# Self-attention's instructions kept in the order of the program, with the first scores ahead of the first values and the comparisons spread over its tiles

## The chip, the core and the metric

The kernel runs on one core of a Trainium2 chip: TensorE (PE, with its weight loads shown apart as PEld), VectorE (DVE), ScalarE (ACT), GpSimd (POOL) and the DMA queues, each with its own list of instructions, tied together by semaphores. The metric is the device time of one execution in microseconds (us), as the median of several runs. A profile comes from one further execution; its span is the time from the first to the last instruction.

## The reference

One layer of a Perceiver: cross-attention, causal self-attention and a feed-forward network whose weights are reduced to -1, 0 and 1, each added to `x` (32 sequences of 64 rows of 512 numbers, all float32). The change lies in the second part and in what prepares the third:

```python
def _L0_attn_ref(x, WQ, WK, WV, WO):
    NUM_HEADS = 16
    D_K = D_MODEL // NUM_HEADS
    ...
    Q, K, V = (heads(WQ), heads(WK), heads(WV))
    score = jnp.einsum('bhqd,bhkd->bhqk', Q, K) / jnp.sqrt(jnp.asarray(D_K, x.dtype))
    score = score + mask
    score = score - jnp.max(score, axis=-1, keepdims=True)
    score = jnp.exp(score)
    score = score / jnp.sum(score, axis=-1, keepdims=True)
    out = jnp.einsum('bhqk,bhkd->bhqd', score, V)
    return out.transpose(0, 2, 1, 3).reshape(B, S, E) @ WO
...
h = jnp.einsum('btd,hd->bth', x, absmean(W_fc))
h = layernorm(jax.nn.gelu(h, approximate=False), ln_w, ln_b)
return jnp.einsum('bth,dh->btd', h, absmean(W_proj))
...
x = x + _L0_attn_ref(_layernorm(x, axis=-1), L0_attn_WQ, L0_attn_WK, L0_attn_WV, L0_attn_WO)
x = x + _L0_ffn_ref(_layernorm(x, axis=-1), L0_ffn_W_fc, L0_ffn_ln_w, L0_ffn_ln_b, L0_ffn_W_proj)
```

`absmean` divides a weight matrix by its mean magnitude and rounds to -1, 0 or 1. In the kernel this is two comparisons of each weight with a threshold.

## The kernel before

`x` stays in SBUF as 16 tiles of 128 rows (two sequences each, `xs[0]` to `xs[15]`). The stages follow each other: queries of the cross-attention, cross-attention (`cross_last`), then `rest`, which holds `self_attention` and `feed_forward`.

Self-attention takes two tiles as a group (GA = 2, eight groups). For a group, `centred_group` normalises the rows of both tiles (`centred`, L107: statistics, mean and variance, scale on DVE, the inverse root on POOL, then `xn` on DVE); `turned_group` transposes them on PE (`atp`) and ACT copies them to SBUF (`axT`). `heads` makes queries, keys and values of a group in six steps: `turned` for half of WQ (`aWQ`, copied by ACT to `QT`), half of WK (`aWK`, copied by DVE to `KT`), and the values of one tile (`aV`, copied by ACT to `V`), and the same once more. It is a generator, and the loop over the tiles takes one of its steps at a time, for the group after the one that is being attended to.

A tile passes through `exponentials` (PE: 16 small products for the scores `sc`; DVE: two operations that scale and mask them into `s`, and the row maximum `amx`; POOL: subtract it; ACT: the exponential), `normalise` (DVE: row sum `atot`, reciprocal, multiply), `turn` (PE: transposes `aptp`; ACT and DVE copy them out to `wo`, whose storage holds the turned probabilities), `mix` (PE: `po`; ACT: `aoT`) and `self_out` (PE: `aout`; DVE adds it to `xs`). The scores of tile i + 1 are made inside tile i, between `mix` and `self_out`.

Two other kinds of work are laid between the tiles. `compare` makes the ternary weights: a DMA on SP's queue fetches one of 32 pieces (`raw_q`, 128x512, in a pool `raw` of two buffers), and two DVE instructions compare it (L869 and L870) into `wf` (first 16 pieces) or `wp`. Three pieces stand in each of the tiles 0 to 10. `ffn_input` (L898) normalises a tile for the feed-forward network (`xn_f`), transposes it on PE (`ftp`) and splits it on DVE into a high and a low part (`fxh`, `fxl`); the first four stand at the end of tiles 5, 7, 9 and 11. In tiles 14 and 15, which have no further group, the steps are the first twelve products of the feed-forward network (`first_hidden`, `fh`; ACT: GELU and square; POOL: sums).

Buffers that matter: `norm` (L90) has two for `xn`, shared by the normalised rows of every stage; `s`, `xT` and `aoT` have one each; the PSUM pool `as_m` has three for all of `aWQ`, `aWK`, `aV`, `atp`, `aptp`, `aout`, `ftp` and `fh`; the scores' PSUM has one [...].

What sets the order: the program is written tile by tile, but the framework's scheduler, when it builds the program, puts each engine's instructions in an order of its own that keeps all dependencies. [...] In the program before, the scheduler moves work forward where it expects an engine to be free: the list of DVE has all 32 pieces compared by the middle of tile 5, row statistics of later groups stand in the cross-attention, and the scores of a tile are often issued in two parts.

Of the kernel before, what the change touches and what calls it, by code (L numbers as in the profile page):

```python
# [18 lines left out]
F32 = mybir.dt.float32  # L19
# [5 lines left out]
ALU = mybir.AluOpType  # L25
# [3 lines left out]
P = 128  # L29
B, T, D = 32, 64, 512  # L30
S = 1601
NT = B * T // P
# [6 lines left out]
GA = 2  # L39
GT = 4  # L40
FC = FF // P
# [39 lines left out]
def perceiver_kernel(ctx: ExitStack, tc: tile.TileContext, a: dict, out: bass.AP):  # L81
    nc = tc.nc
# [6 lines left out]
    small = ctx.enter_context(tc.tile_pool(name="small", bufs=4))  # L89
    norm = ctx.enter_context(tc.tile_pool(name="norm", bufs=2))  # L90
# [16 lines left out]
    def centred(src, gain, eps, name):  # L107

        stats = small.tile([P, 6], F32, tag="stats", name=f"stats_{name}")
        nc.vector.bn_stats(stats, src)  # L110
        mv = small.tile([P, 2], F32, tag="mv", name=f"mv_{name}")
        nc.vector.bn_aggr(mv, stats)
        rs = small.tile([P, 1], F32, tag="rs", name=f"rs_{name}")
        nc.vector.tensor_scalar(rs, mv[:, 1:2], gain, eps, ALU.mult, ALU.add)
        nc.gpsimd.tensor_tensor(rs, rs, neghalf[:, 0:1], ALU.pow)
        xn = norm.tile([P, D], F32, tag="xn", name=f"xn_{name}")
        nc.vector.tensor_scalar(xn, src, mv[:, 0:1], rs, ALU.subtract, ALU.mult)
        return xn

    H = HD // 2  # L120
    wkv = const.tile([P, DC, 2, HD], F32, name="wkv")
# [7 lines left out]
    with ExitStack() as st:  # L129
# [126 lines left out]
        xT = query_input(0)  # L256
# [4 lines left out]
        for g in range(B // 4):  # L261
# [8 lines left out]
            xT = after  # L270
# [612 lines left out]
    def rest(store, measured):  # L883
        st = ExitStack()
        fw = st.enter_context(tc.tile_pool(name="fw", bufs=1))
        wf = fw.tile([P, DC, FF], F32R, name="wf")
        wp = fw.tile([P, FC, D], F32R, name="wp")
        lnw = fw.tile([P, FC], F32, name="lnw")
        lnb = fw.tile([P, FC], F32, name="lnb")
        sums = fw.tile([P, 2, D], F32, name="sums")  # L890
        first = [fw.tile([P, DC, GT * P], F32R, name=f"fx{k}_0") for k in ("h", "l")]

        so_far = [None, None]

        def slot(n):
            return bank[:, n % FC // 4, n % 4 * D : (n % 4 + 1) * D]

        def ffn_input(t, to, ps_t, t_tag):  # L898
            xn = centred(xs[t], 1.0, 1e-5, f"f{t}")
            tp = ps_t.tile([P, DC, P], F32, tag=t_tag, name=f"ftp_{t}")  # L900
            for c in range(DC):
                nc.tensor.transpose(tp[:, c, :], xn[:, c * P : (c + 1) * P], ident)
            at = slice(t % GT * P, (t % GT + 1) * P)
            halves(to[0][:, :, at], to[1][:, :, at], tp)

        def hidden(n, fx, ps_m, m_tag, squares, sq_tag, adder):

            cols = slice(n % FC * P, (n % FC + 1) * P)
            ps = ps_m.tile([P, GT * P], F32, tag=m_tag, name=f"fh_{n}")
            for i, part in enumerate(fx):  # L910
                for c in range(DC):
                    nc.tensor.matmul(  # L912
                        ps,
                        wf[:, c, cols],
                        part[:, c, :],
                        start=(i == 0 and c == 0),
                        stop=(i == 1 and c == DC - 1),
                    )
            g = slot(n)
            nc.scalar.activation(g, ps, AF.Gelu)  # L920
            sq = squares.tile([P, D], F32, tag=sq_tag, name=f"fsq_{n}")
            nc.scalar.activation(sq, g, AF.Square)  # L922
            if n % FC == 0:
                so_far[:] = g, sq
            else:
                nc.gpsimd.tensor_tensor(sums[:, 0], so_far[0], g, ALU.add)  # L926
                adder.tensor_tensor(sums[:, 1], so_far[1], sq, ALU.add)  # L927
                so_far[:] = sums[:, 0], sums[:, 1]

        with ExitStack() as sa:  # L930
            done = self_attention(sa, wf, wp, first, ffn_input, hidden, measured)
        feed_forward(st, wp, lnw, lnb, sums, first, slot, ffn_input, hidden, done, store)
        st.close()

    def self_attention(st, wf, wp, first, ffn_input, hidden, measured):

        raw = st.enter_context(tc.tile_pool(name="raw", bufs=2))
        p1 = st.enter_context(tc.tile_pool(name="a1", bufs=1))
# [1 line left out]
        ps_m = st.enter_context(tc.tile_pool(name="as_m", bufs=3, space=PSUM))  # L940
# [15 lines left out]
            return wf[:, j // 4, j % 4 * D : (j % 4 + 1) * D] if j < FC else wp[:, j - FC, :]  # L956

        def centred_group(g):
            return [centred(xs[g * GA + t], 1.0, 1e-5, f"a{g}_{t}") for t in range(GA)]

        def turned_group(g, xns):
            xT = p1.tile([P, DC, GA * P], F32, tag="xT", name=f"axT_{g}")
            for t, xn in enumerate(xns):
                tp = ps_m.tile([P, DC, P], F32, tag="mm", name=f"atp_{g}_{t}")
                for c in range(DC):
                    nc.tensor.transpose(tp[:, c, :], xn[:, c * P : (c + 1) * P], ident)
                nc.scalar.copy(xT[:, :, t * P : (t + 1) * P], tp)  # L967
            return xT

        made = {}  # L970

        def heads(g, xT):


            QT = p2.tile([P, DC, GA * P], F32, tag="QT", name=f"QT_{g}")
            KT = p2.tile([P, DC, GA * P], F32, tag="KT", name=f"KT_{g}")
            V = p2.tile([P, GA, D], F32, tag="V", name=f"V_{g}")
            made[g] = QT, KT, V

            def turned(w, dst, m0, copy):  # L980
                ps = ps_m.tile([P, 2, GA * P], F32, tag="mm", name=f"a{w}_{g}_{m0}")
                for m in range(2):
                    for c in range(DC):
                        nc.tensor.matmul(  # L984
                            ps[:, m, :],
                            ws[w][:, c, (m0 + m) * P : (m0 + m + 1) * P],
                            xT[:, c, :],
                            start=(c == 0),
                            stop=(c == DC - 1),
                        )  # L990
                copy(dst[:, m0 : m0 + 2, :], ps)  # L991

            for i in range(GA):
                turned("WQ", QT, 2 * i, nc.scalar.copy)
                yield
                turned("WK", KT, 2 * i, nc.vector.tensor_copy)
                yield
                ps = ps_m.tile([P, D], F32, tag="mm", name=f"aV_{g}_{i}")
                for c in range(DC):
                    nc.tensor.matmul(  # L1000
                        ps,
                        xT[:, c, i * P : (i + 1) * P],
                        ws["WV"][:, c, :],
                        start=(c == 0),
                        stop=(c == DC - 1),
                    )
                nc.scalar.copy(V[:, i, :], ps)
                yield

        def first_hidden():  # L1010
# [82 lines left out]
            nc.vector.tensor_tensor(xs[i], ps, xs[i], ALU.add)  # L1093


        chores = {i: range(3 * i, min(3 * i + 3, 2 * FC)) for i in range(11)}
        groups = NT // GA
        xT = turned_group(0, centred_group(0))
        for _ in heads(0, xT):
            pass  # L1100
        thresholds(ps_m)
        s = exponentials(0)
        xT = turned_group(1, centred_group(1))
        xns = None
        for i in range(NT):
            g, t = divmod(i, GA)
            if t == 0:
                steps = heads(g + 1, xT) if g + 1 < groups else first_hidden()
            next(steps)
            normalise(i, s)  # L1110
            next(steps)
            if t == 0 and g + 2 < groups:
                xns = centred_group(g + 2)
            turn(i, s)
            next(steps)
            oT = mix(i)
            if i + 1 < NT:
                s = exponentials(i + 1)
            self_out(i, oT)
            for j in chores.get(i, ()):  # L1120
                compare(raw, j, piece_of(j))
            if t == GA - 1 and g + 2 < groups:
                xT = turned_group(g + 2, xns)
            if i in (5, 7, 9, 11):
                ffn_input((i - 5) // 2, first, ps_m, "mm")
        return 12

    def feed_forward(st, wp, lnw, lnb, sums, first, slot, ffn_input, hidden, done, store):
        fx = st.enter_context(tc.tile_pool(name="fx", bufs=1))
        ft = st.enter_context(tc.tile_pool(name="ft", bufs=3))  # L1130
        fq = st.enter_context(tc.tile_pool(name="fq", bufs=2))
# [1 line left out]
        ps_m = st.enter_context(tc.tile_pool(name="fs_m", bufs=2, space=PSUM))  # L1133
# [79 lines left out]
        for n in range(last):  # L1213
# [21 lines left out]
                others(g, c - 10)  # L1235
            if n in inputs_at:
                t = inputs_at[n]
                ffn_input(t, inputs[t // GT % 2], ps_t, "tp")
            if c == FC - 1:
                for t in range(GT):  # L1240
                    i = g * GT + t
# [112 lines left out]
```

## Time and profile before

| what | us |
|---|---|
| median of 3 runs | 984.78 (983.76 to 987.26) |
| the profiled execution | 985.89 |
| its span | 984.1 |
| PE busy | 906.7 (92%) |
| DVE busy | 651.9 (66%) |
| ACT busy | 306.8 (31%) |
| POOL busy | 293.1 (30%) |
| first `aWQ` of self-attention | 387.3 |
| first `fh` | 685.1 |
| last `aout` starts | 724.2 |

"Busy" is the share of the span in which an engine had an instruction running. In the rows below, a group of instructions is named by its line, engine and operation, with output <- inputs by the program's names, and the number of instructions after an x; a pair of brackets holds the time that the engine sat idle before it and what ended that. In a row of the waits, the numbers are the total in us, how often, and the longest. The costs of the instructions at hand, by their usual duration in the trace:

| instruction | engine | us each |
|---|---|---|
| `s`, one half of the rows (L1033) | DVE | 1.22 |
| `amx`, `atot` (L1042, L1051) | DVE | 1.22, 1.21 |
| normalising product (L1053) | DVE | 1.22 |
| first and second comparison (L869, L870) | DVE | 0.48, 0.75 |
| row statistics (L110) | DVE | 0.68 |
| `xn` (L117) | DVE | 0.54 |
| `fxh`, `fxl` (L876, L877) | DVE | 0.68, 0.68 |
| copy of keys (L991) | DVE | 0.69 |
| subtract of the maximum (L1043) | POOL | 1.90 |
| exponential (L1046) | ACT | 1.06 |

### The profile page before, as it was taken

To read this page: it belongs to the slowest core of one execution; us is meant where nothing else is said; L and a number is where in the kernel's file an instruction comes from. 1 tells how busy PE (TensorE), PEld (TensorE's weight loads), DVE (VectorE), ACT (ScalarE), POOL (GpSimd) and SP (SyncE) were. 2 spreads that over 40 slices of the span, in tenths; PEclk is the share of its full clock that TensorE was granted. 3 is DMA by queue.
4 is the path that set the end of the run, shared out by engine and by line. 5 is a ranking of instruction groups with operands and counts; after the bars stand their busy time and mean duration, and the time that the engine had idled before them with its cause. 6 is when DMAs were issued, how large, how long until landed. Compare 5 with 4: busy or idle time off the path is not lost.

```text
span 984.1 us, 13369 instructions
## 1 busy us (share of the span) xinstructions
PE 906.7 (92%) x4694; PEld 672.1 (68%) x4694; DVE 651.9 (66%) x1209; ACT 306.8 (31%) x694; POOL 293.1 (30%) x264
## 2 busy tenths in 40 slices
PE   4997889999999999988989999999979899999995
PEld 2786667777677766755566766766647688888884
DVE  4994456656565443499976666666439798886864
ACT  1112345455454532122222222222622233333330
POOL 3554222323222221011011111111757454443330
PEclk9999899999999999999999999999999999999998
DMA  6266664876776550023310000000000010010101
GB/s 198 65 206 168 196 190 136 278 235 206 235 208 213 149 182 24 21 86 87 87 43 1 1 1 1 1 2 1 1 1 1 1 43 1 1 44 1 43 1 46
DMA packets 60964, 83.74 MB, mean 85 GB/s; under 512 B 11060, under 2 KB 34136, under 8 KB 60888
## 3 DMA queue, kind: packets, MB, share of 16 engines
q1 hardware_dynamic: 57568, 80.60, 27.3%
q10 hardware_dynamic: 3320, 2.20, 0.7%
q8 instruction: 39, 0.64, 0.3%
q14 instruction: 37, 0.30, 0.1%
HBM read 74.38 MB, written 4.19 MB: 80 GB/s over the span
## 4 chain that ended last, share of the span: by engine, by line
PE 62%; DVE 14%; POOL 4%; issue 3%; DMA 3%; ACT 3%; SPq 1%; POOLq 0%; DVEq 0%; ACTq 0%
PE y L1225 10%; PE fh L912 10%; PE kvp L382 9%; PE aV L1000 5%; PE xo L504 5%; PE aWQ L984 4%; PE aWK L984 4%; PE lgp L424 3%; PE enc L488 3%; DVE s L1033 3%; DMA nat<-in_ctx_dram 2%; PE aout L1090 2%; PE po L1076 1%; DVE amx L1042 1%; PE sc L1028 1%
## 5 line engine op out<-in xcount | busy, mean ns | idle before, releaser
L382 PE MATMUL kvp<-wkv,ct 128*128 128x256 f32 x576 | 140.8, 391 | 4.4 <-ACT kv L389 4.4
L382 PEld LDWEIGHTS kvp<-wkv,ct 128*128 128x128 f32 x576 | 111.5, 197 | 27.9 <-issue 7.3
L926 POOL TENSOR_TENSOR sums<-sums,bank 128x512 f32<-128x512 f32 x56 | 77.2, 1378 | 90.9 <-ACT bank L920 90.7
L1225 PE MATMUL y<-wp,hTh 128*128 128x512 f32 x256 | 102.7, 401 | 0.6 <-DVE hTh L1204 0.6
L1225 PE MATMUL y<-wp,hTl 128*128 128x512 f32 x256 | 100.7, 393 | 0.7 <-DVE hTl L1205 0.7
L1043 POOL TENSOR_TENSOR s<-s,amx 128x1024 f32<-128x1024 f32 x16 | 30.6, 1913 | 226.0 <-DVE amx L1042 226.0
L920 ACT ACTIVATE bank<-fh 128x512 f32<-128x512 f32 x64 | 38.1, 599 | 154.0 <-PE fh L912 154.0
L912 PE MATMUL fh<-fxh,wf 128*128 128x512 f32 x256 | 73.1, 407 | 6.3 <-issue 4.8
L912 PE MATMUL fh<-fxl,wf 128*128 128x512 f32 x256 | 71.4, 401 | 0.0
L1033 DVE SCALAR_TENSOR_TENSOR s<-sc,cmask 64x1024 f32<-64x1024 f32 x32 | 39.1, 1222 | 44.5 <-PE sc L1028 44.1
L927 DVE TENSOR_TENSOR sums<-sums,fsq 128x512 f32<-128x512 f32 x46 | 54.6, 1186 | 19.5 <-ACT fsq L922 19.4
L1000 PE MATMUL aV<-bank,axT 128*128 128x512 f32 x128 | 62.2, 631 | 4.4 <-DVE KT L991 4.4
L389 ACT ACTIVATE kv<-kvp,rstd 128x256 f32<-128x256 f32 x72 | 33.2, 469 | 92.8 <-PE kvp L382 54.6
L504 PE MATMUL xo<-wo,encT 128*128 128x512 f32 x128 | 59.7, 609 | 2.1 <-ACT encT L497 2.0
L1090 PE MATMUL aout<-bank,aoT 128*128 128x512 f32 x128 | 59.2, 605 | 0.7 <-ACT aoT L1084 0.7
L984 PE MATMUL aWQ<-axT,bank 128*128 128x256 f32 x256 | 58.3, 381 | 1.5 <-ACT axT L967 1.5
L912 PEld LDWEIGHTS fh<-fxh,wf 128*128 128x128 f32 x256 | 47.1, 190 | 18.3 <-issue 6.8
L1205 DVE SCALAR_TENSOR_TENSOR hTl<-bank,lnw,hTh 128x512 fp32r<-128x512 f32 x64 | 55.9, 874 | 5.3 <-PE y L1225 1.1
L191 PE MATMUL q<-xT,wq 128*128 128x256 f32 x256 | 58.2, 386 | 0.0
L984 PE MATMUL aWK<-axT,bank 128*128 128x256 f32 x256 | 57.9, 379 | 0.0
L1225 PEld LDWEIGHTS y<-wp,hTh 128*128 128x128 f32 x256 | 48.2, 188 | 13.8 <-DVE hTh L1204 1.4
L912 PEld LDWEIGHTS fh<-fxl,wf 128*128 128x128 f32 x256 | 48.9, 191 | 12.5 <-issue 0.8
(156 smaller groups left out, 1625.9 us busy)
## 6 DMA issues: line engine op xcount, KB each, us to landing
nat<-in_ctx_dram SPq DMA_DIRECT2D x64, 256.0 KB, 5.1
ct<-in_ctxT_dram SPq DMA_DIRECT2D x7, 768.0 KB, 4.8
xraw<-in_x_dram SPq DMA_DIRECT2D x16, 256.0 KB, 2.7
x<-in_x_dram SPq DMA_DIRECT2D x32, 128.0 KB, 4.9
qs<-bank SPq DMA_DIRECT2D x32, 128.0 KB, 3.1
raw_g<-in_W_fcT_dram SPq DMA_DIRECT2D x16, 256.0 KB, 3.7
raw_g<-in_W_projT_dram SPq DMA_DIRECT2D x16, 256.0 KB, 4.4
raw_q<-in_W_fcT_dram SPq DMA_DIRECT2D x16, 256.0 KB, 3.0
```

What stands on the lines that cost most here:

```text
L191: nc.tensor.matmul(ps.rearrange("p b t -> p (b t)"), wq[:, c, h, :], xT[:, c, :], start=(c == 0), stop=(c == DC - 1),)
L382: nc.tensor.matmul(ps.rearrange("p k h -> p (k h)"), cts[p][:, c, j * P : (j + 1) * P], wkv[:, c].rearrange("p k h -> p (k h)"), start=(c ...
L504: nc.tensor.matmul(o, encT[:, h].rearrange("p s t -> p (s t)"), wo[:, h, :], start=(h == 0), stop=(h == NH - 1),)
L912: nc.tensor.matmul(ps, wf[:, c, cols], part[:, c, :], start=(i == 0 and c == 0), stop=(i == 1 and c == DC - 1),)
L926: nc.gpsimd.tensor_tensor(sums[:, 0], so_far[0], g, ALU.add)
L927: adder.tensor_tensor(sums[:, 1], so_far[1], sq, ALU.add)
L984: nc.tensor.matmul(ps[:, m, :], ws[w][:, c, (m0 + m) * P : (m0 + m + 1) * P], xT[:, c, :], start=(c == 0), stop=(c == DC - 1),)
L1000: nc.tensor.matmul(ps, xT[:, c, i * P : (i + 1) * P], ws["WV"][:, c, :], start=(c == 0), stop=(c == DC - 1),)
L1033: nc.vector.scalar_tensor_tensor(s[half], sc[half, :, :, half].rearrange("p r m k -> p (r m) k"), DK**-0.5, cmask[half].unsqueeze(1).to_br ...
L1090: nc.tensor.matmul(ps, oT[:, c, :], ws["WO"][:, c, :], start=(c == 0), stop=(c == DC - 1))
L1205: nc.vector.scalar_tensor_tensor(lo, g, w, hi.bitcast(F32), ALU.mult, ALU.subtract)
L1225: nc.tensor.matmul(ys[t], part[:, t, :], wp[:, c, :], start=(c == 0 and i == 0), stop=(c == FC - 1 and i == 1),)
```

## The change

Five things are changed. `centred_all` takes the place of `centred` for a group: all statistics of both tiles first, then both normalised tiles. `in_order` is called at the end of self-attention: it goes through the instructions emitted since the first group was transposed, and ties each one on PE, DVE, ACT and POOL to the one before it on the same engine, without a semaphore, so that the scheduler keeps the order of the program there. SP's queue is not tied, and instructions emitted after self-attention may still be put between. In the first group, the six steps of `heads` run in another order, so that the scores of tile 0 come before both `aV`; the second group is normalised after the first step. In the loop, a group is normalised after `turn` instead of before it, and transposed ahead of `mix` instead of after the comparisons; `ffn_input` is split, so that the transposes and the split into two parts (`ffn_turned`) come one tile later than the normalising. The 32 comparisons are spread over 14 tiles: two in each of the tiles 0 to 7, three in 8 to 11, two in 12 and 13.

```diff
+    def centred_all(srcs, gain, eps, name):
+        mvs, rss, xns = [], [], []
+        for k, src in enumerate(srcs):
+            stats = small.tile([P, 6], F32, tag="stats", name=f"stats_{name}_{k}")
+            nc.vector.bn_stats(stats, src)
...
+            nc.gpsimd.tensor_tensor(rs, rs, neghalf[:, 0:1], ALU.pow)
...
+        for k, src in enumerate(srcs):
+            xn = norm.tile([P, D], F32, tag="xn", name=f"xn_{name}_{k}")
+            nc.vector.tensor_scalar(xn, src, mvs[k][:, 0:1], rss[k], ALU.subtract, ALU.mult)
+            xns.append(xn)
+        return xns
+
+    def in_order(begin):
+        before = {}
+        kinds = (mybir.EngineType.PE, mybir.EngineType.DVE, mybir.EngineType.Activation, mybir.EngineType.Pool)
+        for ins in nc.cur_bb.bb.instructions[begin:]:
+            if ins.engine not in kinds or isinstance(ins, mybir.BassTileRelease):
+                continue
+            if ins.engine in before:
+                tc.add_manual_dep(
+                    ins,
+                    before[ins.engine],
+                    mybir.DependencyInfo(mybir.DependencyClass.NoSync, mybir.DependencyReason.DATA),
+                    reason="in order",
+                )
+            before[ins.engine] = ins.name
...
-        def ffn_input(t, to, ps_t, t_tag):
-            xn = centred(xs[t], 1.0, 1e-5, f"f{t}")
+        def ffn_input(t):
+            return centred(xs[t], 1.0, 1e-5, f"f{t}")
+
+        def ffn_turned(t, xn, to, ps_t, t_tag):
             tp = ps_t.tile([P, DC, P], F32, tag=t_tag, name=f"ftp_{t}")
...
-            return [centred(xs[g * GA + t], 1.0, 1e-5, f"a{g}_{t}") for t in range(GA)]
+            return centred_all([xs[g * GA + t] for t in range(GA)], 1.0, 1e-5, f"a{g}")
...
-            for i in range(GA):
-                turned("WQ", QT, 2 * i, nc.scalar.copy)
-                yield
-                turned("WK", KT, 2 * i, nc.vector.tensor_copy)
-                yield
...
+            for k in order:
+                if k % 3 == 0:
+                    turned("WQ", QT, 2 * (k // 3), nc.scalar.copy)
+                elif k % 3 == 1:
+                    turned("WK", KT, 2 * (k // 3), nc.vector.tensor_copy)
+                else:
+                    values(k // 3)
                 yield
...
-        chores = {i: range(3 * i, min(3 * i + 3, 2 * FC)) for i in range(11)}
+        ends = [0, 2, 4, 6, 8, 10, 12, 14, 16, 19, 22, 25, 28, 30, 32]
+        chores = {i: range(*ends[i : i + 2]) for i in range(NT - 2)}
...
-        for _ in heads(0, xT):
-            pass
+        begin = len(nc.cur_bb.bb.instructions)
+        for k, _ in enumerate(heads(0, xT, (0, 1, 3, 4, 2, 5))):
+            if k == 0:
+                xns = centred_group(1)
+            if k == 3:
+                s = exponentials(0)
         thresholds(ps_m)
-        s = exponentials(0)
-        xT = turned_group(1, centred_group(1))
+        xT = turned_group(1, xns)
...
+            turn(i, s)
             if t == 0 and g + 2 < groups:
                 xns = centred_group(g + 2)
-            turn(i, s)
             next(steps)
+            if t == GA - 1 and g + 2 < groups:
+                xT = turned_group(g + 2, xns)
             oT = mix(i)
...
-            if t == GA - 1 and g + 2 < groups:
-                xT = turned_group(g + 2, xns)
             if i in (5, 7, 9, 11):
-                ffn_input((i - 5) // 2, first, ps_m, "mm")
+                fxn = ffn_input((i - 5) // 2)
+            if i in (6, 8, 10, 12):
+                ffn_turned((i - 6) // 2, fxn, first, ps_m, "mm")
+        in_order(begin)
         return 12
```

More of the change, by code (lines that the diff above doesn't have):

```diff
@@ L118, in centred @@
         return xn
+    def centred_all(srcs, gain, eps, name):
[3 more added lines that the diff above has]
+            nc.vector.bn_stats(stats, src)
+            mv = small.tile([P, 2], F32, tag="mv", name=f"mv_{name}_{k}")
+            nc.vector.bn_aggr(mv, stats)
+            rs = small.tile([P, 1], F32, tag="rs", name=f"rs_{name}_{k}")
+            nc.vector.tensor_scalar(rs, mv[:, 1:2], gain, eps, ALU.mult, ALU.add)
+            nc.gpsimd.tensor_tensor(rs, rs, neghalf[:, 0:1], ALU.pow)
+            mvs.append(mv)
+            rss.append(rs)
+        for k, src in enumerate(srcs):
[17 more added lines that the diff above has]
+            before[ins.engine] = ins.name
     H = HD // 2
@@ L930, in rest, with self_attention @@
         with ExitStack() as sa:
-            done = self_attention(sa, wf, wp, first, ffn_input, hidden, measured)
-        feed_forward(st, wp, lnw, lnb, sums, first, slot, ffn_input, hidden, done, store)
+            done = self_attention(sa, wf, wp, first, ffn_input, ffn_turned, hidden, measured)
+        feed_forward(st, wp, lnw, lnb, sums, first, slot, ffn_input, ffn_turned, hidden, done, store)
         st.close()
-    def self_attention(st, wf, wp, first, ffn_input, hidden, measured):
+    def self_attention(st, wf, wp, first, ffn_input, ffn_turned, hidden, measured):
         raw = st.enter_context(tc.tile_pool(name="raw", bufs=2))
@@ L970, in self_attention, with heads @@
         made = {}
-        def heads(g, xT):
+        def heads(g, xT, order=range(6)):
             QT = p2.tile([P, DC, GA * P], F32, tag="QT", name=f"QT_{g}")
@@ L991, in turned, with values @@
                 copy(dst[:, m0 : m0 + 2, :], ps)
-            for i in range(GA):
-                turned("WQ", QT, 2 * i, nc.scalar.copy)
-                yield
-                turned("WK", KT, 2 * i, nc.vector.tensor_copy)
-                yield
+            def values(i):
                 ps = ps_m.tile([P, D], F32, tag="mm", name=f"aV_{g}_{i}")
@@ L1121, in self_attention, with feed_forward @@
                 compare(raw, j, piece_of(j))
-            if t == GA - 1 and g + 2 < groups:
-                xT = turned_group(g + 2, xns)
             if i in (5, 7, 9, 11):
-                ffn_input((i - 5) // 2, first, ps_m, "mm")
+                fxn = ffn_input((i - 5) // 2)
+            if i in (6, 8, 10, 12):
+                ffn_turned((i - 6) // 2, fxn, first, ps_m, "mm")
+        in_order(begin)
         return 12
-    def feed_forward(st, wp, lnw, lnb, sums, first, slot, ffn_input, hidden, done, store):
+    def feed_forward(st, wp, lnw, lnb, sums, first, slot, ffn_input, ffn_turned, hidden, done, store):
         fx = st.enter_context(tc.tile_pool(name="fx", bufs=1))
@@ L1237, in feed_forward @@
                 t = inputs_at[n]
-                ffn_input(t, inputs[t // GT % 2], ps_t, "tp")
+                ffn_turned(t, ffn_input(t), inputs[t // GT % 2], ps_t, "tp")
             if c == FC - 1:
```

## Prediction

> **What bounds the kernel now.** I read the clock and span first (one core, clock 0.98, span 984.1 us), then the chain that ended last, then busy time in stretches of a tile, then TensorE's waits, then the instructions of single tiles in order of time. The chain says TensorE, with VectorE second:
>
> ```profile
> PE 62%; DVE 14%; POOL 4%; issue 3%; DMA 3%; ACT 3%; SPq 1%; POOLq 0%; DVEq 0%; ACTq 0%
> ```
>
> Self-attention runs from 387 us (first aWQ) to 728 us (last aout). Four stretches of it, about a tile each; columns are length, then busy time (and count) of PE, its weight loads, DVE, ACT and POOL, then clock:
>
> ```profile
> 411.00:430.00 19.00, 15.28 (x104) 10.55 (x108) 17.08 (x29) 4.21 (x9) 4.39 (x3) 0.91 0.26 84
> 454.00:475.00 21.00, 17.16 (x118) 11.62 (x117) 19.77 (x36) 5.22 (x10) 3.21 (x3) 0.92 0.34 88
> ...
> 553.00:572.00 19.00, 19.00 (x126) 12.53 (x125) 11.24 (x14) 4.28 (x8) 1.90 (x1) 1.00 0.00 1
> 572.00:590.00 18.00, 16.77 (x129) 12.11 (x127) 12.84 (x25) 5.35 (x10) 3.53 (x4) 1.00 0.00 1
> ```
>
> Early tiles are filled by VectorE (17.08 of 19.00 us) and PE has holes; after 510 us PE is full in odd tiles and loses about 1.2 us in even ones. PE's waits in 382 to 727 us name the holes:
>
> ```profile
> PE aptp L1063 <- DVE s L1053: 6.8, 5, 3.4
> PE ftp L902 <- DVE xn_f L117: 5.0, 4, 1.3
> PE aV L1000 <- DVE KT L991: 4.4, 4, 1.9
> PE sc L1028 <- DVE s L1033: 1.6, 2, 1.0
> ```
>
> One late tile without extra work is the ruler for all that follows (VectorE's rows, then one of POOL, then two of PE):
>
> ```profile
> 515.15 2.46 DVE L1033 SCALAR_TENSOR_TENSOR s<-sc,cmask 64x1024 f32<-64x1024 f32 x2 [4.06 <-PE sc L1028]
> 517.71 1.22 DVE L1042 TENSOR_REDUCE amx<-s 128x16 f32<-128x1024 f32 x1
> 518.96 0.69 DVE L1093 TENSOR_TENSOR x<-aout,x 128x512 f32<-128x512 f32 x1
> 522.10 1.22 DVE L1051 TENSOR_REDUCE atot<-s 128x16 f32<-128x1024 f32 x1 [2.45 <-ACT s L1046]
> 523.64 1.22 DVE L1053 TENSOR_TENSOR s<-s,atot 128x1024 f32<-128x1024 f32 x1
> 519.07 1.90 POOL L1043 TENSOR_TENSOR s<-s,amx 128x1024 f32<-128x1024 f32 x1 [12.82 <-DVE amx L1042]
> 514.13 0.95 PE L1028 MATMUL sc<-KT,QT 32*128 32x128 f32 x24
> 525.46 1.04 PE L1063 MATMUL aptp<-ident,s 128*128 128x128 f32 x8
> ```
>
> Call the end of the scores e (515.08). VectorE's row sum (atot) starts at e+7.02, the normalised scores are there at e+9.78, and PE, after aout, aWQ and aWK, wants them at e+10.38. So VectorE may be 0.60 us late, no more (1.09 where a ftp of 0.49 stands in between). Between amx and atot it is free only while POOL subtracts and ACT takes the exponential. And this freedom is worth less than it looks:
>
> ```profile
> 435.16 0.69 DVE L1093 TENSOR_TENSOR x<-aout,x 128x512 f32<-128x512 f32 x1
> 435.77 1.95 DVE L870 SCALAR_TENSOR_TENSOR wf<-raw_q,thr,wf 128x512 fp32r<-128x512 f32 x1
> 435.27 1.90 POOL L1043 TENSOR_TENSOR s<-s,amx 128x1024 f32<-128x1024 f32 x1 [11.93 <-DVE amx L1042]
> ```
>
> A comparison's second half, 0.75 us elsewhere, takes 1.95 beside POOL's subtract and ends 0.55 after it.
>
> [...] after a hole of 3.41 us the stretch
>
> ```profile
> 423.20:426.60 3.40, 3.40 (x6) 1.42 (x5) 3.31 (x8) 1.23 (x4) 0.14 (x1) 0.50 0.11 31
> ```
>
> has clock 0.50, which costs 1.7 us, and a hole of 2.81 us at 715.5 was followed by po at 1.92 instead of 1.08.
>
> **The change, part by part.** I take TensorE's bare time from the trace, from aWQ of group 1 (411.31) to the first fh (685.5): two tiles take 34.26 (538.94 to 573.20), a pair of atp 0.97, a ftp 0.49; 7x34.26 + 6x0.97 + 4x0.49 = 247.6. It now takes 274.2, so 26.6 is holes, half clock and scores issued in two parts. The new order could win all that. It gives back what VectorE's fixed order makes late:
>
> *First group.* aV goes behind the scores (2x3.45 off their path); aWK ends at 401.4, KT copied 402.15, scores 402.8, exponential ready 409.8. But ACT's copies of V now stand behind that exponential, and the three PSUM buffers hold atp for them: atp ends 411.45, its copies 412.15, so aWQ of group 1 starts at 412.2: 0.9 later. The 3.4 us hole at the first aptp goes (in the 26.6).
>
> *Two comparisons per tile (0 to 4).* After x (e+4.57) the first half waits for POOL (ends e+5.89), is done at e+6.16, then 0.75, and 1.18 for the second: atot at e+8.04 instead of 7.02. Less the 0.60: 0.4 per tile, 2.1 for five.
>
> *FFN input in tiles 5 and 7.* stats 0.68, mv 0.17, rs 0.15, POOL's power 0.55, xn_f 0.53 and their gaps, 2.2 us, all ahead of atot: 2.7 each, 5.4.
>
> *Three comparisons in tiles 8 to 11.* raw has two buffers, so the third load waits for the first comparison (e+6.94) and lands 2.6 to 2.9 us later (from the end of L870 to the start of the L869 that waited, at 473 and 495): done e+10.95 instead of 8.12. Tile 9, with FFN input: 5.5. In tile 11 the row statistics of later FFN tiles also come forward, outside the fixed order (three stats, two rs, one xn_f: 1.3): 6.8.
>
> *The shared xn buffer, tiles 6, 8, 10.* xn (L116) has two buffers for both uses. Now xn_f of the tile before is read by ftp only at the end of this tile, while the second xn_a of the next group wants its buffer in the middle; in the changed program that xn_a waits for TensorE, and the scores' s and x behind it need no wait of their own. So VectorE stands from about 5.5 us after aptp until ftp ends, e+4.08, and s, free at e+0.07, follows xn_a: s to e+7.1, amx 8.42, POOL 10.46, two comparisons 12.69, ftp's two casts 13.99, scores ready 16.67 against 10.87: 5.8 for tile 6. With the third comparison and its load 2.9 more: 8.7 for 8 and for 10. Sum 23.2. Nothing hides this: ACT and POOL wait for the same s.
>
> *Tiles 12 and 13.* Two comparisons, casts 1.3, early stats and xn_f 1.05: 2.3; tile 13: 0.3, under four fh.
>
> Sum of holes: 2.1+5.4+12.3+23.2+2.6 = 45.6. *Half clock:* surely after tiles 6, 8, 9, 10, 11 (holes over 4 us), 5x1.7; after 5, 7, 12 (2.3 to 2.7 us) I take half: 2.5. Bounds for it are 0 and 8x1.7 = 13.6; taken 11.0. So 56.6 against 26.6: +30.0.
>
> *Tail.* fh, squares and copies in order: the last scores come about 0.5 later, but fh 11 no longer splits po, whose end moves from 723.5 to about 721 relative to the first fh. Bounds -4 and +2, taken -1.5. *Row statistics* of groups 2 to 4 leave the cross stage, where they lie beside TensorE (no stats row in its chain): 0, bound -1. SP's list is unchanged in order; its loads follow the comparisons.
>
> Sum: 0.9 + 30.0 - 1.5 = +29.4. The profiled run is 985.89 (span 984.1 and 1.8 around it), giving 1015.3; on the median 984.78 this is 1014.2.
>
> **Rivals.** (a) *The buffer wait is short*, because ftp comes early or the wait stands for an older read: then tile 6 costs 1.2, 8 and 10 cost 4.0 each; 14 less, and 3 of half clock: 997. Against it: s and x carry no wait behind it. (b) *The loads and the clock don't bite*: the third raw is there in time (4x1.6) and half clock costs 5: 1002. [...] (c) *The other side: VectorE's small work does fit under POOL and ACT.* If comparisons and FFN inputs cost nothing there and only the buffer wait stays, 3x3.5 = 10.5, the holes of today go: -26.6 + 10.5 + 0.9 - 1.5 = -16.7: 968. It decides once the mean lateness over 14 tiles is under 27.2/14 = 1.9 us; I have 4.0 with half clock. For it: late tiles leave VectorE 5 to 8 us idle each (18.00-12.84, 19.00-11.24); against: the idle time lies before s, not between amx and atot, where 1.95 instead of 0.75 was seen. (d) *The order does nothing*: excluded by the changed lists on PE, DVE and ACT.
>
> **How the numbers follow.** Forecast 0.62, (a) 0.13, (b) 0.12, (c) 0.13. The forecast's own range is 1005 to 1024; down to 993 it takes in (a) and (b), so about 0.8 lies in 993 to 1024. About 0.3% is what this measurement can tell from no change: faster 0.12, same 0.02, slower 0.86.
>
> **What would show it.** Right: the second xn_a of tiles 6, 8 and 10 idle for some 5 us <- PE ftp; aptp L1063's group waiting over 35 us <- DVE s; a DMA wait at every third comparison of tiles 8 to 11; clock near 0.9 there; no ftp or KT waits; tiles 0 to 4 some 17.5 us each. Wrong: aptp waiting under 20 us in all, or a tail or cross stage moved by over 4 us.

## The result and the profile after

| what | before | after |
|---|---|---|
| median | 985.46 (983.76 to 992.16, 6 runs) | 1015.94 (1015.23 to 1019.91, 6 runs) |
| ratio to before, 95% interval | | 1.0298, 1.0266 to 1.0331 |
| the profiled execution, its span | 985.89, 984.1 | 1015.99, 1014.1 |
| mean granted clock | 0.980 | 0.971 |
| first `aWQ` of self-attention | 387.3 | 382.9 |
| first `aWQ` of group 1 to first `fh` ("the stage" below) | 273.8 | 304.4 |
| first `fh` to `sides` (the tail) | 45.4 | 46.6 |
| `sides` to the end | 253.6 | 255.0 |

The changed kernel is 3.0% slower, and the stage alone is 30.6 us longer. In the profile of the changed kernel, the chain that ended last has less TensorE in it (56% for 62%) and more VectorE (21% for 14%):

```profile
PE 56%; DVE 21%; POOL 4%; issue 3%; ACT 3%; DMA 2%; SPq 0%; DVEq 0%; POOLq 0%; ACTq 0%
```

The first of TensorE's waits from 382 to 760 us in the changed kernel (total us, times, longest):

```profile
PE aptp L1103 <- DVE s L1093: 40.2, 14, 7.1
PE aWK L1020 <- DVE x L1133: 5.1, 3, 1.7
PE fh L948 <- ACT bank L956: 3.7, 2, 2.4
```

One wait now outweighs all others: the transposes of the scores wait for VectorE's normalising product in 14 tiles, 40.2 us instead of 6.8. The waits of `ftp` for `xn_f` and of `aV` for `KT` (5.0 and 4.4 before) are gone. VectorE's own waits in the same time have one that before didn't have, and one that has changed its place:

```profile
DVE xn_a L134 <- PE ftp L938: 15.9, 3, 6.9
DVE wp L903 <- DMA raw_q<-in_W_projT_dram: 5.8, 4, 1.5
```

Before, VectorE stood for loads of pieces as long in sum, 6.0 us:

```profile
DVE wf L869 <- DMA raw_q<-in_W_fcT_dram: 3.4, 4, 1.5
DVE wp L869 <- DMA raw_q<-in_W_projT_dram: 2.6, 3, 1.4
```

Those waits lay in the first tiles. The four of the changed kernel lie between maximum and row sum of tiles 8 to 11.

Tile 6 shows both how the lateness begins and how it grows. These are VectorE's rows in order (start, length, and in brackets the idle time before):

```profile
537.40 0.55 DVE L134 TENSOR_SCALAR xn_a<-x,mv_a,rs_a 128x512 f32<-128x512 f32 x1 [4.49 <-PE ftp L938]
537.96 2.46 DVE L1073 SCALAR_TENSOR_TENSOR s<-sc,cmask 64x1024 f32<-64x1024 f32 x2
540.45 1.22 DVE L1082 TENSOR_REDUCE amx<-s 128x16 f32<-128x1024 f32 x1
541.70 0.69 DVE L1133 TENSOR_TENSOR x<-aout,x 128x512 f32<-128x512 f32 x1
542.31 1.69 DVE L903 TENSOR_SCALAR wf<-raw_q,thr 128x512 fp32r<-128x512 f32 x1
544.04 0.75 DVE L904 SCALAR_TENSOR_TENSOR wf<-raw_q,thr,wf 128x512 fp32r<-128x512 f32 x1
544.71 0.48 DVE L903 TENSOR_SCALAR wf<-raw_q,thr 128x512 fp32r<-128x512 f32 x1
545.22 0.75 DVE L904 SCALAR_TENSOR_TENSOR wf<-raw_q,thr,wf 128x512 fp32r<-128x512 f32 x1
545.89 0.68 DVE L910 CAST fxh<-ftp 128x512 fp32r<-128x512 f32 x1
546.61 0.69 DVE L911 TENSOR_TENSOR fxl<-ftp,fxh 128x512 fp32r<-128x512 f32 x1
547.22 1.21 DVE L1091 TENSOR_REDUCE atot<-s 128x16 f32<-128x1024 f32 x1
```

The second `xn_a` stands 4.49 us until `ftp` has read the shared buffer; behind it in the list wait the scores' `s`, which carry no idle time of their own: the last product of the scores ends at 533.22, and `s` starts at 537.96. Then, between maximum and row sum, the first comparison takes 1.69 instead of 0.48 beside POOL's subtract, and `atot` follows the last cast without a gap: VectorE is the late one, not the exponential. What TensorE makes of it in the next tile:

```profile
542.45 3.72 PE L1020 MATMUL aWK<-axT,bank 128*128 128x256 f32 x16 [1.71 <-DVE x L1133]
550.12 1.94 PE L1103 MATMUL aptp<-ident,s 128*128 128x128 f32 x8 [3.95 <-DVE s L1093]
551.85 5.44 PE L1032 MATMUL aV<-bank,axT 128*128 128x512 f32 x8
557.12 1.04 PE L1002 MATMUL atp<-ident,xn_a 128*128 128x128 f32 x8
558.09 1.08 PE L1116 MATMUL po<-wo,V 128*32 128x128 f32 x32
```

It stands 1.71 and 3.95 us (`aWK` takes the PSUM buffer of `aout`, which `x` has to read first), and afterwards runs slowly: `aV` takes 5.44 instead of 3.60, and from `aptp` to `po` it is 7.97 us, where a tile without a long hole takes 5.33 (4.46 without `atp`). The granted clock says the same. Behind this hole it is 0.50 for 3.4 us; behind a hole of 2.55 us, at the `aptp` of tile 8, it is 1.00 (columns as in the prediction):

```profile
550.12:553.50 3.38, 3.38 (x10) 2.40 (x11) 1.73 (x4) 1.13 (x4) 0.00 (x0) 0.50 0.00 0
573.40:576.80 3.40, 3.40 (x14) 2.04 (x15) 1.91 (x5) 1.46 (x4) 0.00 (x0) 1.00 0.00 0
```

Below, the hole "after tile i" is the time that TensorE stands for VectorE ahead of the `aptp` of tile i + 1, and slow work is the time from that `aptp` to `po` beyond 5.33 or 4.46 us.

### The profile page after: what moved, and what is told of

Its sections match the earlier page's. It is cut to its first block, busy times and chain, and to the rows that moved or that the text cites. A ratio compares the mean times of both kernels' runs of the same rounds, so it can differ in the third digit from the quotient of the medians.

```text
span 1014.1 us, 13372 instructions
## 1 busy us (share of the span) xinstructions
PE 906.8 (89%) x4694; PEld 671.9 (66%) x4694; DVE 665.1 (66%) x1209; ACT 306.7 (30%) x694; POOL 293.8 (29%) x264
## 4 chain that ended last, share of the span: by engine, by line
PE 56%; DVE 21%; POOL 4%; issue 3%; ACT 3%; DMA 2%; SPq 0%; DVEq 0%; POOLq 0%; ACTq 0%
PE y L1272 10%; PE fh L948 10%; PE kvp L416 10%; PE xo L538 5%; PE aV L1032 4%; DVE s L1073 4%; PE enc L522 3%; PE lgp L458 3%; DVE amx L1082 2%; PE aptp L1103 2%; DVE wf L903 2%; DVE s L1093 2%; DVE atot L1091 1%; PE sc L1068 1%; PE po L1116 1%
## 5 line engine op out<-in xcount | busy, mean ns | idle before, releaser
L1032 PE MATMUL aV<-bank,axT 128*128 128x512 f32 x128 | 64.9, 656 | 0.0
L1103 PE MATMUL aptp<-ident,s 128*128 128x128 f32 x128 | 21.6, 324 | 40.2 <-DVE s L1093 40.2
```

Of the source, the lines that this page charges most:

```text
L1032: nc.tensor.matmul(ps, xT[:, c, i * P : (i + 1) * P], ws["WV"][:, c, :], start=(c == 0), stop=(c == DC - 1),)
```

## The experiments

All are measured like the result, each against runs of the kernel before on the same chip, in 4 to 20 executions. Chips and sets differ: the medians of the kernel before lie between 985.5 and 988.1, so that a difference of some 3 us between medians of two sets says nothing, and the ratio is the safer measure. Stage, holes and tail are those of one profiled execution. Times are in us; "holes" are the waits of `aptp` for `s` and of `aWK` for `x` together.

| kernel | median | ratio to before (95%) | stage | holes | tail |
|---|---|---|---|---|---|
| before | 985.5 | 1 | 273.8 | 6.8 | 45.4 |
| after | 1015.9 | 1.0298 (1.0266 to 1.0331) | 304.4 | 45.3 | 46.6 |
| e2_free_order | 980.4 | 0.9944 (0.9922 to 0.9966) | 266.4 | 11.3 | 45.5 |
| e6_dve_free | 986.4 | 0.9983 (0.9967 to 0.9999) | 272.5 | 13.3 | 45.6 |
| e1_own_xn | 1004.5 | 1.0162 (1.0096 to 1.0228) | 289.9 | 31.8 | 47.0 |
| e12_ffn_turn | 994.0 | 1.0093 (1.0064 to 1.0122) | 278.0 | 25.5 | 49.0 |
| e3_compare_after_turn | 985.6 | 0.9968 (0.9946 to 0.9990) | 270.8 | 17.7 | 46.0 |
| e8_third_raw | 1014.7 | 1.0284 (1.0231 to 1.0337) | 298.2 | 39.3 | 47.8 |
| e11_fill | 1023.6 | 1.0389 (1.0357 to 1.0422) | 305.2 | 15.7 | 47.7 |
| e4_all_after_turn | 986.7 | 0.9994 (0.9968 to 1.0021) | 276.4 | 23.1 | 45.6 |
| e5_spread | 982.9 | 0.9952 (0.9932 to 0.9973) | 262.3 | 3.3 | 52.3 |
| e7_spread_free | 974.1 | 0.9850 (0.9804 to 0.9896) | 261.6 | 9.2 | 45.9 |
| e9_spread_more | 976.6 | 0.9889 (0.9837 to 0.9940) | 258.7 | 6.6 | 48.5 |
| e10_tail_free | 976.0 | 0.9883 (0.9832 to 0.9933) | 258.8 | 6.7 | 48.8 |

### Is it the order?

e2_free_order:

```diff
-        in_order(begin)
         return 12
```

> The changed kernel with in_order left out, everything else as it is: the scheduler may again move instructions past each other. Theory (it is the fixed order on VectorE that makes the scores late, the other edits cost little): small work moves behind the row sum again, and the time is 978 to 990. Rival (the spread comparisons and the split FFN input are what costs, in any order): 1005 to 1016.

e6_dve_free:

```diff
-        kinds = (mybir.EngineType.PE, mybir.EngineType.DVE, mybir.EngineType.Activation, mybir.EngineType.Pool)
+        kinds = (mybir.EngineType.PE, mybir.EngineType.Activation, mybir.EngineType.Pool)
```

> The changed kernel with the order fixed on TensorE, ScalarE and GpSimd but not on VectorE. Theory (only VectorE's order costs): about the time without any order, 976 to 988. Rival (TensorE's or ScalarE's fixed order keeps the holes): 1000 to 1016.

Both medians lie where the theory had them. Without the order the rest of the change is 0.56% faster than before; with the order on all engines but VectorE it is about level with it. So the fixed order costs 3.5% of the time before, and most of that is VectorE's list. The first of TensorE's waits, first in e2_free_order:

```profile
PE aptp L1103 <- DVE s L1093: 11.3, 4, 3.7
```

and in e6_dve_free:

```profile
PE aptp L1103 <- DVE s L1093: 13.3, 8, 4.0
```

The same wait shrinks from 40.2 to 11.3 and 13.3 us. With VectorE's order left to the scheduler, which may then place the small work anew, the spreading of the comparisons and the split of the FFN input do no harm.

### The shared buffer and the FFN input

e1_own_xn gives `xn_f` of self-attention storage that is free since the cross-attention (that of `wkv`):

```diff
-    def centred(src, gain, eps, name):
+    def centred(src, gain, eps, name, xn=None):
...
-        xn = norm.tile([P, D], F32, tag="xn", name=f"xn_{name}")
+        if xn is None:
+            xn = norm.tile([P, D], F32, tag="xn", name=f"xn_{name}")
...
+        spare = wkv.rearrange("p (s c) k h -> p s (c k h)", s=2)
...
-                fxn = ffn_input((i - 5) // 2)
+                fxn = ffn_input((i - 5) // 2, spare[:, 0])
```

> The changed kernel (1015.9) with one edit: the normalised FFN input of tiles 5, 7, 9 and 11 has a buffer of its own, so the next group's second xn_a no longer waits for ftp. Theory (the buffer wait is 14 us of the holes, and half clock follows it): the xn_a stalls of 15.9 us go, the aptp holes after tiles 6, 8 and 10 fall from 5.7, 8.3 and 8.4 to about 1, 4 and 4, and perhaps one half clock of 1.7 with them: 1000 to 1003. Rival (the wait only fills time in which VectorE would wait for the scores anyway, or another wait takes its place): 1012 to 1016.

In this kernel VectorE has no wait of `xn_a` for `ftp` at all. TensorE's rows of `aptp` in tiles 7 to 12:

```profile
552.54 1.07 PE L1104 MATMUL aptp<-ident,s 128*128 128x128 f32 x8 [1.25 <-DVE s L1094]
573.12 1.09 PE L1104 MATMUL aptp<-ident,s 128*128 128x128 f32 x8 [2.56 <-DVE s L1094]
596.33 1.94 PE L1104 MATMUL aptp<-ident,s 128*128 128x128 f32 x8 [3.89 <-DVE s L1094]
622.10 1.97 PE L1104 MATMUL aptp<-ident,s 128*128 128x128 f32 x8 [5.22 <-DVE s L1094]
645.35 1.49 PE L1104 MATMUL aptp<-ident,s 128*128 128x128 f32 x8 [4.05 <-DVE s L1094]
672.19 1.97 PE L1104 MATMUL aptp<-ident,s 128*128 128x128 f32 x8 [7.13 <-DVE s L1094]
```

The holes after tiles 6, 8 and 10 are 1.25, 3.89 and 4.05 instead of 5.66, 8.33 and 8.35 (the waits of `aWK` among them): 13.2 less, and about the 1, 4 and 4 that were expected. The stage is 14.5 shorter; by the ratios the gain is 1.4% of the time before, with intervals that don't meet. The median, 1004.5, is a little above the range given, and the slow work did not fall with the holes: 11.3 us, against 11.4 in the changed kernel.

e12_ffn_turn moves the FFN input on top of that:

```diff
             turn(i, s)
+            if i in (5, 7, 9, 11):
+                fxn = ffn_input((i - 5) // 2, spare[:, 0])
...
-            if i in (5, 7, 9, 11):
-                fxn = ffn_input((i - 5) // 2, spare[:, 0])
```

> The kernel with the FFN input's own buffer (e1_own_xn) with one more edit: the FFN input of tiles 5, 7, 9 and 11 is measured and normalised behind the tile's turn and not behind x and the comparisons. Theory (it cost 2.2 to 2.7 per tile between maximum and row sum, and fits behind the turn, where no row statistics stand in odd tiles): the holes after tiles 5, 7, 9 and 11 (2.6, 2.6, 5.2, 7.1) fall by 2.2 or more each and one half clock goes: 10 to 13 below that kernel, 991 to 996. Rival (behind the turn it makes the next scores late by as much): within 3 us of it.

The median is in the range of the theory, 10.5 below that of e1_own_xn, and the stage is 11.9 shorter. By the ratios, though, the gain is only 0.7% of the time before, and their intervals overlap. Nor is it quite the theory's way. The holes after tiles 5, 7, 9 and 11 fell by 2.29, 2.29, 2.26 and 1.26, those after 6, 8 and 10 grew by 1.8 in all (the rival has this part), 6.3 less together. The rest of the 11.9 us in the stage is slow TensorE work that no longer follows: 11.3 us in e1_own_xn and 5.7 here.

### The comparisons and their loads

e3_compare_after_turn:

```diff
             turn(i, s)
+            for j in chores.get(i, ()):
+                compare(raw, j, piece_of(j))
...
-            for j in chores.get(i, ()):
-                compare(raw, j, piece_of(j))
```

> The changed kernel with one edit: the comparisons of a tile are placed behind its turn, where VectorE waits for the next scores (4.06 us in the tile of the ruler), and not behind x, between maximum and row sum. Order stays fixed. Theory (place, not amount): holes of tiles 0 to 4 go to 0.3 or less (-2), tiles 5, 7 and 12 lose about 1.5 each, 6 loses 2, 8 to 11 lose about 4 each, half clock falls by 4 or so: 984 with 978 to 992. Rival (VectorE's amount of work is the bound, so that what leaves one gap makes the scores late in the other): 1008 to 1016.

The same 32 comparisons, in the same tiles and in fixed order, cost 30 us less when they stand where VectorE waits for the scores. Here place decides, not amount. One part went against the theory: in tiles 0, 2 and 4, where the row statistics of the next group stand behind the turn too, the holes grew from at most 0.91 us to between 2.05 and 2.08, while those after tiles 1 and 3 went to nothing. This saving and that of the two kernels above overlap: 33.6 us in the stage here and 26.4 there are more than the 56.7 between the changed kernel's stage (304.4) and TensorE's bare time (247.7), so part of one saving is the other's too; how they share it wasn't tried.

e8_third_raw:

```diff
-            for j in chores.get(i, ()):
-                compare(raw, j, piece_of(j))
+            for k, j in enumerate(chores.get(i, ())):
+                compare(raw, j, piece_of(j), spare[:, 0] if k == 2 else None)
```

(`compare` loads into the buffer given, if there is one.)

> The changed kernel with one edit: the third comparison of tiles 8 to 11 has a buffer of its own for its load, so the load no longer waits for the first comparison. Theory (the load wait stands on the path): the four waits of 1.4 to 1.5 us go, the holes after tiles 8, 9, 10 and 11 (8.3, 5.3, 8.4, 7.1) fall by about 1.5 each, half clock stays: 1008 to 1011. Rival (the wait is hidden by POOL's subtract and the exponential anyway): 1014 to 1017.

In the profile it is as expected: VectorE's four waits for a load are gone, and TensorE's waits show the 6.0 us:

```profile
PE aptp L1108 <- DVE s L1098: 34.2, 14, 5.6
PE aWK L1025 <- DVE x L1138: 5.1, 3, 1.7
```

The holes after tiles 9 and 11 are 3.74 and 5.57 instead of 5.33 and 7.07. The medians don't show it: a gain of 1.2 us, and the intervals of the two ratios overlap (the profiled execution, 1011.4, was the fastest of four). The load wait is on the path by the trace; what it is worth in the time of a run stays open.

### The half clock

e11_fill fills the long holes with products that nothing reads:

```diff
+        fill = {7: 6, 9: 11, 10: 8, 11: 11, 12: 12}
...
             next(steps)
+            if i in fill:
+                ps = ps_o.tile([P, D], F32, tag="po", name=f"fill_{i}")
+                for k in range(fill[i]):
+                    nc.tensor.matmul(ps, ident, ws["WV"][:, 0, :], start=True, stop=True)
             turn(i, s)
```

> The changed kernel with TensorE kept at work in the five long holes: ahead of the first aptp of tiles 7, 9, 10, 11 and 12 stand 6, 11, 8, 11 and 12 more matmuls of 128x512 (about 0.46 us each) into the accumulator of po, which nothing reads. Holes stay as long as they were, only filled. Theory (the half clock comes of the idle time and costs 1.7 to 1.8 after each of them): every aV of these tiles takes 3.60 again, and the time falls by 7 to 9 us, to 1007 to 1009. Rival (the half clock is a throttle that more work doesn't lift, or the slowed aV lies beside other waits): 1014 to 1019.

The time missed both expectations, in part because the filling was too long: a product of 128x512 is two instructions in the trace and took 0.88 us, not 0.46. From the start of `aWK` to `aptp` the five tiles take 1.04, 2.64, 1.39, 2.64 and 3.06 us more than in the changed kernel, 10.8 in all. The stage is nevertheless only 0.8 longer. TensorE's rows of tile 7 say why, beside those of tile 6 in the same kernel:

```profile
529.70 1.09 PE L1103 MATMUL aptp<-ident,s 128*128 128x128 f32 x8 [2.55 <-DVE s L1093]
530.62 5.30 PE L1032 MATMUL aV<-bank,axT 128*128 128x512 f32 x8
...
550.82 5.31 PE L1160 MATMUL fill<-bank,ident 128*128 128x512 f32 x12
555.97 1.04 PE L1103 MATMUL aptp<-ident,s 128*128 128x128 f32 x8
556.84 3.60 PE L1032 MATMUL aV<-bank,axT 128*128 128x512 f32 x8
```

And the clock of the filled hole of tile 7:

```profile
550.80:556.00 5.20, 5.20 (x14) 2.26 (x13) 4.47 (x6) 0.00 (x0) 0.00 (x0) 1.00 0.27 96
```

After a filled hole `aptp` and `aV` take 1.04 and 3.60 in all five tiles, as the theory said; from `aptp` to `po` that is 11.7 us less than in the changed kernel. After the unfilled hole of 2.55 us in tile 6 `aV` takes 5.30 (1.7 us lost; in the changed kernel nothing followed the same hole). 10.8 - 11.7 + 1.7 = 0.8. So in these five tiles the slow work came of the idle time: with products in the hole, the loss of 1.80 to 2.88 us behind each was gone. The rest of this kernel's extra time, 7.0 of 7.8 us between the spans, lies outside the stage (3.1 ahead of it, 3.9 behind) and isn't explained by these rows.

### Dealing the work out to both gaps

e4_all_after_turn is e3_compare_after_turn with the buffer of e1_own_xn and the FFN input behind the turn:

```diff
             turn(i, s)
+            for j in chores.get(i, ()):
+                compare(raw, j, piece_of(j))
+            if i in (5, 7, 9, 11):
+                fxn = ffn_input((i - 5) // 2, spare[:, 0])
             if t == 0 and g + 2 < groups:
                 xns = centred_group(g + 2)
...
-            for j in chores.get(i, ()):
-                compare(raw, j, piece_of(j))
-            if i in (5, 7, 9, 11):
-                fxn = ffn_input((i - 5) // 2)
```

> The changed kernel with three edits: own buffer for the FFN input, comparisons behind the turn, and the FFN input's statistics and normalisation behind the turn too. Nothing extra is left between maximum and row sum but x. Theory: aptp holes of 40.2 us fall under 10, half clock under 4, which leaves TensorE's bare time: 963 to 972. Rival (the order behind the turn is as tight, s comes late instead): 985 or more, with the chain of waits showing s behind comparisons.

The theory missed by 15 us; the rival was right. VectorE's rows of tile 8, behind the turn:

```profile
572.20 0.49 DVE L904 TENSOR_SCALAR wp<-raw_q,thr 128x512 fp32r<-128x512 f32 x1
...
576.15 0.49 DVE L904 TENSOR_SCALAR wp<-raw_q,thr 128x512 fp32r<-128x512 f32 x1 [1.49 <-DMA raw_q<-in_W_projT_dram]
...
580.34 0.55 DVE L135 TENSOR_SCALAR xn_a<-x,mv_a,rs_a 128x512 f32<-128x512 f32 x1 [0.44 <-POOL rs_a L130]
580.90 2.46 DVE L1074 SCALAR_TENSOR_TENSOR s<-sc,cmask 64x1024 f32<-64x1024 f32 x2
```

Three comparisons, a load and two normalisations take 8.7 us (572.20 to 580.90) where the ruler's gap is 4.06, and `s` is late instead of `atot`. The gap has a size.

e5_spread deals the work out by size:

```diff
+        turn_n = dict.fromkeys(range(12), 1) | {5: 0, 7: 0, 9: 0, 11: 0, 12: 3, 13: 3, 14: 2, 15: 2}
+        late_n = dict.fromkeys(range(NT), 1) | {2: 2, 4: 2, 6: 0, 8: 0, 10: 0, 12: 0}
...
             turn(i, s)
-            if t == 0 and g + 2 < groups:
-                xns = centred_group(g + 2)
+            beside(i)
...
-            for j in chores.get(i, ()):
-                compare(raw, j, piece_of(j))
-            if i in (5, 7, 9, 11):
-                fxn = ffn_input((i - 5) // 2)
+            comparisons(i, late_n[i])
```

(`beside(i)` measures and normalises one tile of the group after next, and the FFN input in its tiles, with `turn_n[i]` comparisons between.)

> The changed kernel with VectorE's small work dealt out to the two gaps by their size, in fixed order. Behind the turn (4.06 us in the ruler) of tiles 0 to 11 one normalisation of the next group and one comparison, or, in tiles 5, 7, 9 and 11, the FFN input instead of the comparison; behind x one comparison, none where the FFN input is turned and two in tiles 2 and 4; the remaining 14 comparisons in tiles 12 to 15, with two spare buffers so that no load is late. Theory (each gap holds what fits into it at no cost): aptp and aWK holes under 8 us in all, half clock under 2, so 960 to 970. Rival (both gaps together are already full, VectorE is the bound in fixed order): 980 to 990.

e7_spread_free is the same without `in_order`:

> The kernel with the small work dealt out to both gaps, and no fixed order. Theory (the scheduler moves instructions out of the gaps again, as it does in the changed kernel without order): 972 to 985, slower than the same in fixed order. Rival (place in the program is enough, order is not needed): within 4 us of it.

Both theories missed. The 982.9 of e5_spread lies in its rival's range, but not for the rival's reason, as the stage shows. TensorE's first waits there:

```profile
PE atp L1023 <- DVE xn_a L151: 9.6, 6, 2.2
PE fh L969 <- ACT bank L977: 6.2, 4, 2.2
PE aptp L1124 <- DVE s L1114: 3.3, 4, 1.6
```

The waits for the scores are nearly gone (3.3 us), and the stage, 42.1 us shorter than in the changed kernel, shows it. But the second `xn_a` of a group now comes late for `atp`, and the tail is 5.7 us longer: in tiles 14 and 15, in which the program has POOL sum `fh`, the second half of a comparison takes up to 1.66 us, against 0.75 in all twelve rows from 422 to 506 us. The scheduler, left free with the same program, keeps the stage (261.6) and has no such tail (45.9): fixed order is not needed for the gain, and here loses 8.9 us against it. The rival of e7_spread_free (within 4 us) missed as well.

e9_spread_more puts `atp` behind `po` and takes the comparisons out of the last two tiles, by other numbers in `turn_n` and `late_n`; e10_tail_free also ends the fixed order ahead of tile 14. The edit of `atp`:

```diff
-            if t == GA - 1 and g + 2 < groups:
-                xT = turned_group(g + 2, xns)
-                xns.clear()
             oT = mix(i)
+            if t == GA - 1 and g + 2 < groups:
+                xT = turned_group(g + 2, xns)
+                xns.clear()
```

> The kernel with the small work dealt out to both gaps, in fixed order, with two more edits: the next group's atp goes behind po instead of ahead of it, and the comparisons of tiles 14 and 15 move to tiles 0 to 5 (two behind x there, two behind the turn of tiles 1 and 3). Theory (what is left of that kernel's loss is 9.6 us of atp waiting for xn_a, and some 6 us that comparisons cost in the last two tiles): 967 to 975. Rival (the waits only change their name, the scores are late by as much): 979 to 984.

> The same with the order fixed only up to tile 13, so that the last two tiles, with the first twelve fh, are left to the scheduler. Theory (in fixed order the tail loses 3 to 6 us, since copies and squares of fh stand behind the exponential): 2 to 6 us under the fixed one. Rival (the tail is bound by TensorE): within 1.5 us of it.

e9_spread_more goes the way of its theory, to 976.6, 1.6 us above the range: the waits of `atp` fall to 2.9 us and the tail to 48.5, but 6.6 us of waits for the scores have come back (3.3 in e5_spread). Freeing the tail brings nothing (the rival). It exchanges one wait for another: `po` then waits 2.8 us for a copy. Three versions, e7_spread_free, e9_spread_more and e10_tail_free, beat both kernels, the kernel before by over 1% at the median; their intervals don't tell them apart.

## Why the prediction was right, point by point

The forecast of +29.4 came out as +30.0 in the profiled spans. Of the signs that it named, those of being right came: `xn_a` idle for 15.9 us in three tiles, `aptp` waiting 40.2 us, a load wait at the third comparison of tiles 8 to 11, a clock of 0.91 to 0.95 over tiles 8 and 9, no waits of `ftp` and `aV` (tiles 0 to 4 took 18.2 us each, not 17.5). But one sign of being wrong came too, a cross stage moved by over 4 us; it is taken up below. The terms:

- **Bare time.** 247.6 was taken for the stage. The changed kernel's 304.4 less its holes (45.3) and its slow work (11.4) is 247.7. For the stage before, the prediction read the first `fh` at 685.5; the row has 685.12, so that 26.2 us, not 26.6, were there to be won.
- **Holes.** Booked 45.6, measured 45.3. Tiles 0 to 4: 2.1, measured 3.1 (0.75, 0.27, 0.91, 0.27, 0.90). Tiles 5 and 7: 5.4, measured 5.1. Tiles 9 and 11: 12.3, measured 12.4. Tiles 6, 8, 10: 23.2, measured 22.3. Tiles 12 and 13: 2.6, measured 2.4.
- **Mechanisms behind them.** Of the 23.2, the buffer wait was said to be 14; e1_own_xn took 13.2 away, and the holes that it leaves, 1.25, 3.89 and 4.05, are the 1.2, 4.0 and 4.0 of rival (a), whose premise the wait of 15.9 us refutes. The third comparison with its load was booked at 2.8 in tile 9; e8_third_raw splits it, in tile 9, into 1.6 of waiting and 1.2 of work (3.74 against 2.55 in a tile without it). The FFN input, 2.2 of the 2.7 booked for its tile, is 2.3 in e12_ffn_turn. The first comparison is held up beside POOL's subtract, 1.69 in place of 0.48.
- **Half clock.** Booked 11.0, the author's estimate from two holes of the kernel before (3.41 us, with a loss of 1.7, and 2.81): five tiles at 1.7 and half of three more. Measured 11.4, from five tiles alone: 2.64, 1.80, 2.88, 1.97 and 2.08, behind holes of 5.66, 8.33, 5.33, 8.35 and 7.07. So the sum is right by luck, and its two factors are not: a mean of 2.3 each, and in this execution nothing after the holes of 2.55, 2.55 and 2.11. The length of the hole alone doesn't decide: one of 2.55 or 2.56 us was followed by an `aV` of 3.60 in the changed kernel (both times), by 5.30 and 3.60 in e11_fill (tiles 6 and 8), and by 5.29 twice in e1_own_xn. What else does was not shown.
- **First group.** Booked +0.9; from the first `aWQ` to that of group 1 it is 25.16 instead of 23.97: +1.2.
- **Tail.** This is a step that failed: -1.5 was booked, +1.2 measured. `po` is no longer split, as said, but `fh` waits 3.7 us for ACT, whose GELUs stand in the fixed order behind squares that wait 2.50 and 1.00 us for POOL's sums, and 1.7 for copies. The last `po` ends 38.3 us after the first `fh`, before 38.4. It lies inside the bounds given.
- **Row statistics leave the cross stage.** Booked 0 with a bound of -1; self-attention began 4.4 us earlier, far outside the bound. Most of this is the clock, which was priced for the stage alone. Two groups of products in the cross stage run slowly before and not after, though the hole ahead of them is the same. The first of them before, in the changed kernel and in e1_own_xn (granted clock over it 0.70 before and 1.00 in the changed kernel):

```profile
106.02 5.25 PE L382 MATMUL kvp<-wkv,ct 128*128 128x256 f32 x16 [2.64 <-ACT kv L389]
105.80 3.72 PE L416 MATMUL kvp<-wkv,ct 128*128 128x256 f32 x16 [2.63 <-ACT kv L423]
107.13 6.78 PE L417 MATMUL kvp<-wkv,ct 128*128 128x256 f32 x16 [2.63 <-ACT kv L424]
```

The second, an `xo` behind a hole of 1.48 us, takes 5.29, 3.60 and 5.14. Together they are 3.2 of the 4.4 us. It is not the row statistics that decide, since e1_own_xn has moved them like the changed kernel (4 of them are left in the cross stage in both, 10 before), and is slow in both places. In the kernels of the table whose edits all lie behind it, the first `aWQ` starts anywhere from 382.7 (e8_third_raw) to 388.3 (e1_own_xn). What decides whether slow work follows a hole stays open, as does the rest of the 4.4. `sides` to the end is 1.5 longer, about the time by which `sides` itself runs slowly (5.42 for 3.87). Start, tail and end, -4.4 + 1.2 + 1.5, come to -1.7, about the -1.5 that was booked for the tail alone; that the sum is so close is luck.

Rival (c), that the small work fits under POOL and ACT, was wrong as to the gap between maximum and row sum, and right as to the tile as a whole: e9_spread_more, in fixed order, reaches 258.7 in the stage, 15.1 less than before.

## What to carry to other kernels

Fixing an engine's order makes each place in the program a promise: count, for every gap of the engine that is not the bound, what the program puts into it and how long the gap is, before tying it down; here moving the same instructions from one gap to another saved 30 us, and filling that other gap with more than it holds cost time again. A ruler taken from one undisturbed tile, with the moment at which the bound engine wants the result, was enough to price the holes of 14 tiles within 1.0 us in each group of tiles, and within 1% in sum, where the errors of the groups partly cancel. Buffers that two uses share have to be looked at again whenever the order of the uses changes, because what stands behind a wait in the fixed order starts late with it: in tile 6 the 4.49 us of `xn_a` held `s`, and with it the scores.

## What the runs showed of the hardware

- The granted clock was 0.50 for 3.4 us behind the hole after tile 6, and TensorE's work there ran slowly. More than the length of the hole ahead decided on such slow work: 2.55 us was followed by none in the changed kernel and by a loss of 1.7 us in e11_fill; the `kvp` behind a hole of 2.63 or 2.64 us took 3.72, 5.25 and 6.78 us in three kernels; a hole of 1.48 us was followed by a loss of 1.7 us before and none after. A loss of up to 2.88 us was seen after a hole of 5.33. Products that nothing reads, put into the hole, prevented it in five tiles of five.
- The start of self-attention lay 5.7 us apart between profiled executions of kernels whose edits lie behind it (382.65 in e8_third_raw, 388.33 in e1_own_xn). Executions of one kernel differ too. Of the kernel before, one took 979.6 us (span) at a mean clock of 0.984 and another 991.1 at 0.974.
- Two VectorE comparisons beside GpSimd's subtract of 1.90 us ended only after it: by 0.55 us before (a second half, 1.95 instead of 0.75 us), by 0.28 in tile 6 of the changed kernel (a first half, 1.69 instead of 0.48).
- A 128x512 product in float32 is two instructions in the trace and took 0.88 us in a row (e11_fill: 12 instructions, six products, in 5.31 us).
